# A depthwise 3x3 convolution in 64x64 tiles, its sums emptied by two engines, its order in a table of slots

## The chip, the cores and the metric

The kernel runs on one core of a Trainium2 chip. A core has five engines with a program of their own each, which meet at semaphores: TensorE (PE, matrix products into the accumulator memory PSUM), VectorE (DVE), ScalarE (ACT), GpSimd (POOL) and SyncE (SP), which starts transfers (DMA). Tensors that are worked on lie in SBUF, the on-chip memory with 128 partitions. The metric is the device time of one launch in microseconds (us), the median of several runs. Beside these runs one execution was taken by the hardware profiler; views and line numbers (L1471 is line 1471 of the kernel before) come from it.

## The reference

The input x has 4 samples of 256 channels and 48x48 points, in fp32. Four layers follow, each of the form x = x + layer(group norm of x): attention with 8 heads, a gate from large depthwise convolutions, single-head attention with a batch norm over all samples, and layer 3, which the change is in:

```python
def _L3_conv_ref(x, attn_w1, attn_w2, refine_w, refine_b):
    p = jnp.mean(x, axis=(2, 3))
    h = jax.nn.leaky_relu(p @ attn_w1.T, SLOPE)
    a = jax.nn.sigmoid(h @ attn_w2.T)
    y = x * a[:, :, None, None]
    y = conv(y, refine_w, padding='SAME', groups=C)      # 3x3, each channel by itself
    y = y + refine_b[None, :, None, None]
    mu = jnp.mean(y, axis=(2, 3), keepdims=True)
    var = jnp.mean(jnp.square(y - mu), axis=(2, 3), keepdims=True)
    y = (y - mu) * rsqrt(var + EPS)
    return jax.nn.leaky_relu(y, SLOPE)
...
x = x + _L2_conv_ref(_gn(x), ...)      # ends in W_w @ y, then the batch norm
x = x + _L3_conv_ref(_gn(x), ...)
```

## The kernel before

A sample has 256 channels, two channel halves (NK = 2) of 128 partitions each, and N = 2304 points. A *slice* is SL = 384 points (8 rows), six to a half (NSL), and a *third* is two slices, GW = 768 points (NG3 = 3). A *tile* of layer 3 is one half of one sample; there are eight, sample after sample in the order SEQ = 1, 2, 3, 0. Samples 1 to 3 lie in SBUF; sample 0 is loaded again into `x_back` (L1290).

Layer 2's last product needs statistics over all four samples, which `w_stats` (L1015) gathers while the attention still runs. So layer 3 begins by computing that product again and adding it to x. This is class `Pre`, in six *steps* per sample: four 64x64 products on TensorE (`product`, L1334), batch norm while ScalarE empties PSUM (`normed`, L1341), the addition to x (`gain`, L1365, mostly on GpSimd), statistics of the sum on VectorE (`stats`, L1370). Then `chain`: small operations on VectorE with four small products on TensorE between them and a reciprocal root on GpSimd (the helper `rsqrt`, L165), which give the group norm's mean and scale and the channel gate. They end in two ScalarE operations that write normed and gated x into a *pad*, a 50x50 image with a zero border (L1433). Four pads rotate.

Class `Conv` is one tile. `products` (L1458) does the first four taps of each slice on TensorE: the weight matrix is a 128x128 diagonal of one tap's weights (`diagonals`, L1045, made by GpSimd during layer 2), the other side a shifted window of the pad, and PSUM adds up. Two slices share a tile of two PSUM banks; three such tiles rotate (`two_banks`). `taps` (L1471) adds the other five taps, each a VectorE scalar_tensor_tensor (window times weight plus what PSUM holds) over a third, in place in PSUM. `evict` (L1477) adds the bias on ScalarE, writes the third `z` to SBUF and sums it. `centre` takes the first third's mean as a shift of origin, `square` (L1490) sums squares on ScalarE; `scales` (L1497 to L1505) are small VectorE operations and a `rsqrt` on GpSimd, `shift` (L1510) a 128x1 operation behind it; `scale` (L1516) norms z on ScalarE, `leak` (L1520) is the leaky relu on VectorE (z times slope, maximum with z: both inputs are z), `gain` (L1524) adds z to x on GpSimd in thirds, `store` (L1527) sends it out. In the last tile these four go third by third, gain on VectorE.

The order is written by hand: in this part of the program every engine executes its instructions as they stand in the code (`manual_schedule`), each behind the semaphore waits that the framework puts in for shared tiles. A loop over tiles and slices (from L1564) interleaves the work of three tiles: products of the present one, taps and norm of the one before, gain and store of the one before that, and one step or chain piece of a later sample. A judge of layer 0's sums (six small operations, value `sound`, read at the very end) stands ahead of it.

Of the kernel before, what the change touches and what calls it, by code (L numbers as in the profile page):

```python
# [9 lines left out]
F32 = mybir.dt.float32  # L10
# [4 lines left out]
P = 128  # L15
HW = 48
# [58 lines left out]
def usual_path(  # L75
# [958 lines left out]
    PE_TAPS = (0, 1, 2, 3)  # L1034
    DVE_TAPS = (4, 5, 6, 7, 8)
    diag = {}

    def diagonals():

        for k in range(NK):  # L1040
            xs = xsp.tile([P, NK, SL + 1], F32, tag="xs", name="diag")
            xs = xs.rearrange("p k s -> p (k s)")[:, : len(PE_TAPS) * P]
            diag[k] = xs.rearrange("p (t j) -> p t j", j=P)
            for n, t in enumerate(PE_TAPS):
                nc.gpsimd.tensor_scalar(  # L1045
                    diag[k][:, n, :], ident, rfw[:, k, t : t + 1], None, ALU.mult
                )
                yield 1
# [258 lines left out]

    W2 = HW + 2
# [5 lines left out]
    GW = 2 * SL  # L1314

# [5 lines left out]
    class Pre:  # L1321


        def __init__(self, n):
            self.n, self.b = n, SEQ[n]
            self.st = small.tile([P, NK, NSL, 6], F32, tag="gn_st", name="gn_st")
            self.steps = [(k, c) for k in range(NK) for c in range(L2C)]
# [25 lines left out]
        def add(self, i):  # L1353
            halves = [pj_tile()[:, :SL] for _ in range(2)]
            self.product(i, halves)
            tmp = wk.tile([P, 2, SL], F32, tag="tmp", name="tmp")
            for h in range(2):
                self.normed(i, tmp[:, h, :], halves[h])
            self.gain(i, tmp, nc.gpsimd)
# [7 lines left out]
        def stats(self, i):  # L1367
            k, c = self.steps[i]
            for s in (c, c + L2C):
                nc.vector.bn_stats(  # L1370
                    self.st[:, k, s, :], X[self.b][:, k, s * SL : (s + 1) * SL]
                )

        def chain(self):

            mv = small.tile([P, NK, 2], F32, tag="gn_mv", name="gn_mv")
            for k in range(NK):
                nc.vector.bn_aggr(mv[:, k, :], self.st[:, k].rearrange("p s f -> p (s f)"))
            yield
            ps = pj_tile()  # L1380
            nc.tensor.matmul(ps[:, 0:NK], lhsT=gmat, rhs=mv[:, :, 0], start=True, stop=True)
            yield
            gm = small.tile([P, NK], F32, tag="gn_gm", name="gn_gm")
            nc.vector.tensor_copy(gm, ps[:, 0:NK])
            dev = small.tile([P, NK], F32, tag="gn_dev", name="gn_dev")
            nc.vector.tensor_sub(dev, mv[:, :, 0], gm)
            sq = small.tile([P, NK], F32, tag="gn_sq", name="gn_sq")
            nc.vector.tensor_mul(sq, dev, dev)
            nc.vector.tensor_add(sq, sq, mv[:, :, 1])
            yield  # L1390
            ps = pj_tile()
            nc.tensor.matmul(ps[:, 0:NK], lhsT=gmat, rhs=sq, start=True, stop=True)
            yield
            gv = small.tile([P, NK], F32, tag="gn_gv", name="gn_gv")
            nc.vector.tensor_scalar(gv, ps[:, 0:NK], GN_EPS, None, ALU.add)
            rs = small.tile([P, NK], F32, tag="gn_rs", name="gn_rs", bufs=6)
            rsqrt(rs, gv)
            yield
            yield

            pm = small.tile([P, NK], F32, tag="pm", name="pm")
            nc.vector.tensor_mul(pm, dev, rs)
            nb = small.tile([P, NK], F32, tag="gn_nb", name="gn_nb", bufs=6)
            nc.vector.scalar_tensor_tensor(nb, gm, -1.0, rs, ALU.mult, ALU.mult)
            yield
            ps = pj_tile()
            for k in range(NK):
                nc.tensor.matmul(
                    ps[0:D, 0:1], lhsT=w1[:, k, :], rhs=pm[:, k : k + 1],
                    start=k == 0, stop=k == NK - 1,  # L1410
                )
            raw = small.tile([D, 1], F32, tag="hraw", name="hraw")
            nc.vector.tensor_copy(raw, ps[0:D, 0:1])
            hl = small.tile([D, 1], F32, tag="hl", name="hl")
            nc.vector.scalar_tensor_tensor(hl, raw, SLOPE, raw, ALU.mult, ALU.max)
            yield
            ps = pj_tile()
            for k in range(NK):
                nc.tensor.matmul(
                    ps[:, k : k + 1], lhsT=w2[:, k * P : (k + 1) * P], rhs=hl,  # L1420
                    start=True, stop=True,
                )

            ga = small.tile([P, NK], F32, tag="ga", name="ga")
            nc.scalar.activation(ga, ps[:, 0:NK], AF.Exp, scale=-1.0)
            nc.vector.tensor_scalar(ga, ga, 1.0, None, ALU.add)
            nc.vector.reciprocal(ga, ga)
            rsa = small.tile([P, NK], F32, tag="rsa", name="rsa")
            nc.vector.tensor_mul(rsa, rs, ga)
            nba = small.tile([P, NK], F32, tag="nba", name="nba")  # L1430
            nc.vector.tensor_mul(nba, nb, ga)
            for k in range(NK):
                nc.scalar.activation(  # L1433
                    pads[(self.n * NK + k) % NPAD][:, 1 : 1 + HW, 1 : 1 + HW],
                    X[self.b][:, k, :].rearrange("p (r c) -> p r c", c=HW), AF.Identity,
                    bias=nba[:, k : k + 1], scale=rsa[:, k : k + 1],
                )
                yield

    class Conv:  # L1440


        def __init__(self, i):
# [3 lines left out]
            self.z = big.tile([P, N], F32, tag="qk"[i // 2 % 2], name="z")  # L1447

            self.st = small.tile([P, 2, NG3], F32, tag="in_st", name="in_st", bufs=3)
            self.ps = {}  # L1450

        def products(self, s):
            g = s // 2
            if s % 2 == 0:
                self.ps[g] = two_banks(self.i * NG3 + g)
            for n, t in enumerate(PE_TAPS):
                dr, dc = divmod(t, 3)
                nc.tensor.matmul(  # L1458
                    self.ps[g][:, s % 2, :SL].rearrange("p (r c) -> p r c", c=HW),
                    lhsT=diag[self.k][:, n, :],  # L1460
                    rhs=self.pad[:, s * RS + dr : (s + 1) * RS + dr, dc : dc + HW],
                    start=n == 0, stop=n == len(PE_TAPS) - 1,
                )

        def taps(self, g):
            z = self.ps[g][:, :, :SL].rearrange("p h (r c) -> p h r c", c=HW)
            for t in DVE_TAPS:
                dr, dc = divmod(t, 3)
                r0 = 2 * g * RS + dr
                src = self.pad[:, r0 : r0 + 2 * RS, dc : dc + HW]  # L1470
                nc.vector.scalar_tensor_tensor(  # L1471
                    z, src.rearrange("p (h r) c -> p h r c", h=2),
                    rfw[:, self.k, t : t + 1], z, ALU.mult, ALU.add,
                )

        def evict(self, g):
            nc.scalar.activation(  # L1477
                self.z[:, g * GW : (g + 1) * GW].rearrange("p (h s) -> p h s", h=2),
                self.ps[g][:, :, :SL], AF.Identity, bias=vec[:, V_RB, self.k : self.k + 1],
                accum_out=self.st[:, 0, g : g + 1],  # L1480
            )
# [53 lines left out]


    ok = lp.tile([P, 2, LW], F32, name="ok")
    nc.vector.tensor_scalar(ok[:, 0, :], lsum, SUM_HI, None, ALU.is_le)
    nc.vector.tensor_scalar(ok[:, 1, :], lmin, SUM_LO, None, ALU.is_ge)
    okm = lp.tile([P, 1], F32, name="okm")  # L1540
    nc.vector.tensor_reduce(okm, ok, AX.XY, ALU.min)
    ps = pj_tile()
    nc.tensor.matmul(ps[0:1, 0:1], lhsT=okm, rhs=ones[:, 0:1], start=True, stop=True)
    sound = lp.tile([1, 1], mybir.dt.int32, name="sound")
    nc.vector.tensor_scalar(sound, ps[0:1, 0:1], P - 0.5, None, ALU.is_ge)

    pres = {0: Pre(0), 1: Pre(1)}
    for i in range(NK * L2C):
# [3 lines left out]
    pres[0].stats(NK * L2C - 1)  # L1552
    _drain(pres[0].chain())


    steps = {}
    for s in range(NSL):
        steps[0, s] = (1, s)
    for b in range(2, B):
        for c in range(L2C):  # L1560
            steps[NK * (b - 2) + 1, 2 * c] = (b, c)
            steps[NK * (b - 1), 2 * c] = (b, L2C + c)

    convs, pending = [], None  # L1564
    for i, (b, k) in enumerate(TILES):
        cv = Conv(i)
        convs.append(cv)
        prev = convs[i - 1] if i else None
# [912 lines left out]
```

## Time and profile before

| what | value |
|---|---|
| median of 3 runs | 3684.39 us (3683.62 to 3686.41) |
| the profiled execution | 3686.69 us |
| its span | 3685.0 us |
| granted TensorE clock, mean | 0.982 |
| first product of layer 3's convolution (L1458) | at 3454.75 us |
| last eviction (L1477) ends | at 3669.92 us |
| last gain (L1524) ends | at 3679.67 us |
| mean of one tap on VectorE (L1471, 128x768) | 1.02 us |

The span is the time from the first to the last record of the profiled execution. A row of the table of groups gives line, engine, operation, output<-inputs with shapes, count, then total busy time in us and mean in ns, and after the second bar the idle time before such operations with what ended it. "The chain" is the work that ended last, followed back from the end. "The waits" add up how long an engine stood for another.

### The profile page before, as it was taken

To read this page: it belongs to the slowest core of one execution; us is meant where nothing else is said; L and a number is where in the kernel's file an instruction comes from. 1 tells how busy PE (TensorE), PEld (TensorE's weight loads), DVE (VectorE), ACT (ScalarE), POOL (GpSimd) and SP (SyncE) were. 2 spreads that over 40 slices of the span, in tenths; PEclk is the share of its full clock that TensorE was granted. 3 is DMA by queue.
4 is the path that set the end of the run, shared out by engine and by line. 5 is a ranking of instruction groups with operands and counts; after the bars stand their busy time and mean duration, and the time that the engine had idled before them with its cause. 6 is when DMAs were issued, how large, how long until landed. Compare 5 with 4: busy or idle time off the path is not lost.

```text
span 3685.0 us, 86525 instructions
## 1 busy us (share of the span) xinstructions
PE 3516.1 (95%) x36338; PEld 1766.9 (48%) x36338; DVE 2520.1 (68%) x3209; ACT 2343.6 (64%) x3814; POOL 1423.6 (39%) x899
## 2 busy tenths in 40 slices
PE   8999999999999999999999999999999999999685
PEld 4554545554444444544444445444444445654343
DVE  3455555476778676767786667667967787576687
ACT  4565666566875885568758856687587555555353
POOL 2333333333343334333433343334333456664232
PEclk9999999999999999999999999999999999999797
DMA  2111111111111111311111111111111100000001
GB/s 90 47 26 22 26 21 25 21 29 18 26 21 25 21 25 21 76 21 25 21 25 21 25 21 25 21 25 21 25 17 25 17 6 6 6 8 4 26 34 70
DMA packets 112959, 95.53 MB, mean 26 GB/s; under 512 B 56128, under 2 KB 110000, under 8 KB 110768
## 3 DMA queue, kind: packets, MB, share of 16 engines
q1 hardware_dynamic: 109952, 87.73, 13.0%
q8 instruction: 286, 4.69, 0.5%
q10 hardware_dynamic: 2608, 2.18, 0.2%
q14 instruction: 113, 0.93, 0.1%
HBM read 56.97 MB, written 11.80 MB: 19 GB/s over the span
## 4 chain that ended last, share of the span: by engine, by line
PE 71%; DVE 14%; issue 6%; ACT 5%; POOL 4%; DMA 1%; SPq 0%; DVEq 0%; ACTq 0%; POOLq 0%
PE sc L246 27%; PE av L266 27%; PE pj L528 6%; DVE acc L292 5%; PE pj L610 3%; PE pj L559 3%; POOL half L277 2%; DVE sc L1471 2%; ACT pt L252 2%; PE pj L299 1%; ACT prod L789 1%; DVE av L1471 1%; PE pj L851 1%; DVE acc L286 1%; PE pj L967 1%
## 5 line engine op out<-in xcount | busy, mean ns | idle before, releaser
L252 ACT ACTIVATE pt<-sc 128x768 f32<-128x768 f32 x1944 | 1476.4, 812 | 790.0 <-PE sc L246 787.5
L277 POOL TENSOR_TENSOR half<-pt 128x768 f32<-128x768 f32 x477 | 939.9, 1972 | 1729.0 <-ACT pt L252 1650.1
L246 PE MATMUL sc<-q,k 64*64 64x384 f32 x13824 | 1280.1, 485 | 9.8 <-ACT pt L252 9.4
L266 PE MATMUL av<-pt,v 64*64 64x384 f32 x13824 | 1280.4, 485 | 0.0
L292 DVE TENSOR_TENSOR acc<-acc,pt 128x768 f32<-128x768 f32 x792 | 885.2, 1118 | 84.4 <-DVE acc L292 2.3
L246 PEld LDWEIGHTS sc<-q,k 64*64 64x64 f32 x13824 | 510.1, 133 | 636.2 <-issue 498.7
L266 PEld LDWEIGHTS av<-pt,v 64*64 64x64 f32 x13824 | 514.7, 133 | 590.7 <-issue 554.8
L292 DVE TENSOR_TENSOR acc<-acc,half 128x768 f32<-128x768 f32 x459 | 473.6, 1032 | 349.2 <-POOL half L277 348.3
L615 DVE SCALAR_TENSOR_TENSOR x<-pj,bo,x 128x384 f32<-128x384 f32 x192 | 118.2, 616 | 512.3 <-PE pj L610 512.0
L789 ACT ACTIVATE prod<-pd,wt 128x256 f32<-128x256 f32 x486 | 280.9, 745 | 0.2
L528 PE MATMUL pj<-xs,w 128*128 128x384 f32 (+1 forms) x720 | 275.4, 505 | 0.0
L347 POOL TENSOR_TENSOR o<-o,rinv 128x384 f32<-128x384 f32 x95 | 125.9, 1326 | 238.7 <-DMA rinv<-rinv 224.5
L528 PEld LDWEIGHTS pj<-xs,w 128*128 128x128 f32 x720 | 124.1, 189 | 127.9 <-issue 38.3
L610 PE MATMUL pj<-o,wo 128*128 128x384 f32 x384 | 160.7, 503 | 22.1 <-DVE x L615 17.9
L266 PE MATMUL av<-pt,qv 64*64 64x384 f32 x1728 | 174.6, 497 | 0.0
L246 PE MATMUL sc<-qv,kd 64*64 64x384 f32 x1728 | 169.7, 486 | 2.4 <-ACT pt L252 2.4
L807 DVE TENSOR_REDUCE prod<-prod 128x256 f32<-128x1280 f32 x114 | 168.6, 1479 | 0.0
L559 PEld LDWEIGHTS pj<-w,xs 128*128 128x128 f32 x1080 | 134.5, 191 | 24.1
L286 DVE TENSOR_TENSOR acc<-pt 128x768 f32<-128x768 f32 x99 | 131.7, 1331 | 12.5 <-ACT pt L252 12.5
L559 PE MATMUL pj<-w,xs 128*128 128x128 f32 x1080 | 134.9, 275 | 0.0
L544 ACT ACTIVATE k<-pj,bias 128x384 f32<-128x384 f32 x90 | 52.2, 580 | 106.6 <-PE pj L528 106.2
L343 POOL TENSOR_TENSOR o<-raw 128x384 f32<-128x384 f32 x95 | 112.2, 1182 | 0.0
(235 smaller groups left out, 2716.6 us busy)
## 6 DMA issues: line engine op xcount, KB each, us to landing
xs<-in_x_dram SPq DMA_DIRECT2D x90, 384.0 KB
rinv<-rinv SPq DMA_DIRECT2D x208, 94.5 KB
out_dram<-x SPq DMA_DIRECT2D x6, 1152.0 KB
l<-row SPq DMA_DIRECT2D x416, 1.5 KB
w<-in_wqkv_dram SPq DMA_DIRECT2D x32, 192.0 KB
x<-in_x_dram SPq DMA_DIRECT2D x5, 1152.0 KB
rinv<-ls SPq DMA_DIRECT2D x208, 1.5 KB
x_out<-x SPq DMA_DIRECT2D x6, 384.0 KB
```

Source lines behind the costliest of these rows:

```text
L246: nc.tensor.matmul(ps[c * D : (c + 1) * D, h, :SL], lhsT=u["of"]["k"][r, j0 : j0 + D], rhs=u["of"]["q"][r, u["qc"]], start=True, stop=True,)
L252: nc.scalar.activation(pt, ps[:, :, :SL], AF.Exp, scale=u["scale"])
L266: nc.tensor.matmul(u["av"][h * D : (h + 1) * D, half, :SL], lhsT=value(u, j, h)[r], rhs=pt[r, h, :], start=j == 0, stop=j == JB - 1,)
L277: nc.gpsimd.tensor_add(half, pts[0], pts[1])
L286: nc.vector.tensor_add(u["acc"], ready[0], ready[1])
L292: nc.vector.tensor_add(u["acc"], u["acc"], term)
L347: eng.tensor_mul(o, o, u["rinv"])
L528: nc.tensor.matmul(ps[:, :n], lhsT=at["w"][:, k, t, :], rhs=xs[s][:, k, :n], start=k == 0, stop=k == NK - 1,)
L559: nc.tensor.matmul(ps[:, i * P : (i + 1) * P], lhsT=xs[s][:, k, i * P : (i + 1) * P], rhs=at["w"][:, k, 2, :], start=k == 0, stop=k == NK - 1,
L610: nc.tensor.matmul(ps[:, :SL], lhsT=wo[:, p, k * P : (k + 1) * P], rhs=o["o"], start=True, stop=True,)
L789: nc.scalar.activation(bufs[n % 3][:, :, min(n, 1) + i].rearrange("p (r c) -> p r c", c=AS), pd[:, PAD + dr : PAD + dr + AS, PAD + dc : PA ...
L807: nc.vector.tensor_reduce(to, bufs[n % 3][:, :, : min(n, 1) + len(taps)], AX.X, ALU.add)
```

## The change

Eight taps (all but the middle one, tap 4) go to TensorE, as 64x64 products: four per pair of taps, one from each half of the partitions to each half. A slice now fills a two-bank tile by itself: bank h holds what came from partition half h, even-numbered taps in the same half of the partitions, odd-numbered ones in the other half. So a channel's sum lies in two places, one of them in the other half of the partitions, and emptying brings them together.

`evict(s)` empties one slice with four operations on 64 partitions: twice VectorE (middle tap times window plus one bank, into z) and twice ScalarE (the other bank plus bias, into `part`, at the other half of the partitions). `join(g)` adds `part` to z over a third and sums it in one tensor_tensor_reduce on VectorE. For the crossed halves a second bias tile `rb_x` is loaded with its halves exchanged. Diagonals are 128x64 and sixteen, from `ident2` (two identities of 64 on top of each other).

The order of all work is a table: `at(t, rank, fn)` puts a function into slot t, one slot per slice, and each slot's functions are issued by rank: FRONT, PRODUCT, CONV, EVICT, SMALL, NEXT, THEN, LAST, OUT. With t the first slot of a tile, its products stand at t to t+5, evictions one slot later, joins at t+3, +5, +7, squares at t+4, +6, +8, scales at t+9, shift at t+10, then scale, leak, gain and store in thirds, two slots apart (the last tile: one). Pads are written in thirds of 17, 16 and 15 rows (`ROWS`). The chain's small products go to columns from SL on of the present slice's first bank (`columns`), in place of tiles of their own. Three steps of the second sample move into the first sample's chain (`FILLED`), and the judge moves to slots 6 and 7.

The chain's operations are the same as before, only split into functions, and `judge` likewise; both bodies are left out here.

```diff
-    PE_TAPS = (0, 1, 2, 3)
-    DVE_TAPS = (4, 5, 6, 7, 8)
+    PE_TAPS, DVE_TAP = (0, 1, 2, 3, 5, 6, 7, 8), 4
     diag = {}
 
     def diagonals():
 
         for k in range(NK):
             xs = xsp.tile([P, NK, SL + 1], F32, tag="xs", name="diag")
-            xs = xs.rearrange("p k s -> p (k s)")[:, : len(PE_TAPS) * P]
-            diag[k] = xs.rearrange("p (t j) -> p t j", j=P)
+            xs = xs.rearrange("p k s -> p (k s)")[:, : len(PE_TAPS) * D]
+            diag[k] = xs.rearrange("p (t j) -> p t j", j=D)
             for n, t in enumerate(PE_TAPS):
                 nc.gpsimd.tensor_scalar(
-                    diag[k][:, n, :], ident, rfw[:, k, t : t + 1], None, ALU.mult
+                    diag[k][:, n, :], ident2, rfw[:, k, t : t + 1], None, ALU.mult
                 )
...
+    rb_x = lp.tile([P, NK], F32, name="rb_x")
+    for to, fr in zip(HALVES, HALVES[::-1]):
+        nc.sync.dma_start(rb_x[to, :], vecs[fr, V_RB, :])
...
+    ROWS = [0, 2 * RS + 1, 4 * RS + 1, HW]
...
-        def add(self, i):
-            halves = [pj_tile()[:, :SL] for _ in range(2)]
-            self.product(i, halves)
-            tmp = wk.tile([P, 2, SL], F32, tag="tmp", name="tmp")
+        def multiply(self, i):
+            self.halves = [pj_tile()[:, :SL] for _ in range(2)]
+            self.product(i, self.halves)
+
+        def evict(self, i):
+            self.tmp = wk.tile([P, 2, SL], F32, tag="tmp", name="tmp")
             for h in range(2):
-                self.normed(i, tmp[:, h, :], halves[h])
-            self.gain(i, tmp, nc.gpsimd)
+                self.normed(i, self.tmp[:, h, :], self.halves[h])
...
+            return [
+                (means, lambda ps: of_groups(ps, of["mv"][:, :, 0])),
+                (squares, lambda ps: of_groups(ps, of["sq"])),
+                (inverse, None), (pooled, first), (hidden, second), (gate, scaled),
+            ]
+        def pad(self, k, i):
+
+            r0, r1 = ROWS[i], ROWS[i + 1]
+            nc.scalar.activation(
+                pads[(self.n * NK + k) % NPAD][:, 1 + r0 : 1 + r1, 1 : 1 + HW],
+                X[self.b][:, k, :].rearrange("p (r c) -> p r c", c=HW)[:, r0:r1, :],
+                AF.Identity, bias=self.nba[:, k : k + 1], scale=self.rsa[:, k : k + 1],
+            )
...
-            self.ps = {}
+            self.ps, self.part = {}, {}
+
+        def window(self, r, s, t):
+            dr, dc = divmod(t, 3)
+            return self.pad[r, s * RS + dr : (s + 1) * RS + dr, dc : dc + HW]
 
         def products(self, s):
+            if s == 0:
+                self.z = big.tile([P, N], F32, tag="qk"[self.i // 2 % 2], name="z")
+
+                self.st = small.tile([P, 2, NG3], F32, tag="in_st", name="in_st", bufs=3)
+            now["ps"] = self.ps[s] = two_banks(self.i * NSL + s)
+            last = len(PE_TAPS) // 2 - 1
+            for n in range(last + 1):
+                for h, r in enumerate(HALVES):
+                    for e in range(2):
+                        nc.tensor.matmul(
+                            self.ps[s][HALVES[h ^ e], h, :SL].rearrange(
+                                "p (r c) -> p r c", c=HW
+                            ),
+                            lhsT=diag[self.k][r, 2 * n + e, :],
+                            rhs=self.window(r, s, PE_TAPS[2 * n + e]),
+                            start=n == 0, stop=n == last,
+                        )
+
+        def evict(self, s):
+
+
+
             g = s // 2
             if s % 2 == 0:
-                self.ps[g] = two_banks(self.i * NG3 + g)
-            for n, t in enumerate(PE_TAPS):
-                dr, dc = divmod(t, 3)
-                nc.tensor.matmul(
-                    self.ps[g][:, s % 2, :SL].rearrange("p (r c) -> p r c", c=HW),
-                    lhsT=diag[self.k][:, n, :],
-                    rhs=self.pad[:, s * RS + dr : (s + 1) * RS + dr, dc : dc + HW],
-                    start=n == 0, stop=n == len(PE_TAPS) - 1,
-                )
-
-        def taps(self, g):
-            z = self.ps[g][:, :, :SL].rearrange("p h (r c) -> p h r c", c=HW)
-            for t in DVE_TAPS:
-                dr, dc = divmod(t, 3)
-                r0 = 2 * g * RS + dr
-                src = self.pad[:, r0 : r0 + 2 * RS, dc : dc + HW]
+                self.part[g] = wk.tile([P, 2, SL], F32, tag="part", name="part")
+            z = self.z[:, s * SL : (s + 1) * SL].rearrange("p (r c) -> p r c", c=HW)
+            for h, r in enumerate(HALVES):
                 nc.vector.scalar_tensor_tensor(
-                    z, src.rearrange("p (h r) c -> p h r c", h=2),
-                    rfw[:, self.k, t : t + 1], z, ALU.mult, ALU.add,
-                )
-
-        def evict(self, g):
-            nc.scalar.activation(
-                self.z[:, g * GW : (g + 1) * GW].rearrange("p (h s) -> p h s", h=2),
-                self.ps[g][:, :, :SL], AF.Identity, bias=vec[:, V_RB, self.k : self.k + 1],
-                accum_out=self.st[:, 0, g : g + 1],
+                    z[r], self.window(r, s, DVE_TAP), rfw[r, self.k, DVE_TAP : DVE_TAP + 1],
+                    self.ps[s][r, h, :SL].rearrange("p (r c) -> p r c", c=HW),
+                    ALU.mult, ALU.add,
+                )
+                nc.scalar.activation(
+                    self.part[g][HALVES[1 - h], s % 2, :], self.ps[s][r, 1 - h, :SL],
+                    AF.Identity, bias=rb_x[r, self.k : self.k + 1],
+                )
+
+        def join(self, g):
+            z = self.z[:, g * GW : (g + 1) * GW]
+            nc.vector.tensor_tensor_reduce(
+                z, z, self.part[g].rearrange("p h s -> p (h s)"), 1.0, 0.0, ALU.add, ALU.add,
+                self.st[:, 0, g : g + 1],
             )
...
+    pres = [Pre(n) for n in range(B)]
+    STEPS = NK * L2C
+    for i in range(STEPS):
         pres[0].first(i, (nc.vector, nc.gpsimd)[i % 2])
         if i:
             pres[0].stats(i - 1)
-    pres[0].stats(NK * L2C - 1)
-    _drain(pres[0].chain())
-
-
-    steps = {}
-    for s in range(NSL):
-        steps[0, s] = (1, s)
-    for b in range(2, B):
-        for c in range(L2C):
-            steps[NK * (b - 2) + 1, 2 * c] = (b, c)
-            steps[NK * (b - 1), 2 * c] = (b, L2C + c)
-
-    convs, pending = [], None
-    for i, (b, k) in enumerate(TILES):
-        cv = Conv(i)
-        convs.append(cv)
-        prev = convs[i - 1] if i else None
-        older = convs[i - 2] if i > 1 else None
-        final = i == len(TILES) - 1
-        rest = iter(())
+    pres[0].stats(STEPS - 1)
+
+    FILLED = 3
+    filled = iter(range(FILLED))
+    for n, part in enumerate(pres[0].chain()):
+        part[0](None)
+        if part[1]:
+            part[1](pj_tile())
+        if n in (1, 2, 4):
+            pres[1].first(next(filled), nc.gpsimd)
+    for i in range(NG3):
+        pres[0].pad(0, i)
...
+    FRONT, PRODUCT, CONV, EVICT, SMALL, NEXT, THEN, LAST, OUT = range(9)
+    events = {}
+
+    def at(t, rank, fn):
+        events.setdefault(t, []).append((rank, fn))
...
+    def columns():
+
+        return now["ps"][:, 0, SL:]
+
+    def put_chain(t, parts):
+        for dt, (head, tail) in enumerate(parts):
+            at(t + dt, FRONT, lambda fn=head: fn(None))
+            if tail:
+                at(t + dt, SMALL, lambda fn=tail: fn(columns()))
+
+    def put_step(t, n, i, gap=1):
+        at(t, PRODUCT, lambda: pres[n].multiply(i))
+        at(t, NEXT, lambda: pres[n].evict(i))
+        at(t, OUT, lambda: pres[n].gain(i, pres[n].tmp, nc.gpsimd))
+        at(t + gap, LAST, lambda: pres[n].stats(i))
+
+    for i in range(NG3):
+        at(2 + i, LAST, lambda i=i: pres[0].pad(1, i))
+    for i in range(FILLED):
+        at(i // 2, LAST, lambda i=i: pres[1].stats(i))
+    for i in range(FILLED, STEPS):
+        put_step(i - FILLED, 1, i)
+    put_chain(6, judge())
+    SAMPLE = NK * NSL
+    for n in range(1, B):
+        t = (n - 1) * SAMPLE
+        if n > 1:
+            for i in range(STEPS):
+                put_step(t - 9 + 2 * i, n, i)
+        put_chain(t + 4, pres[n].chain())
+        for k in range(NK):
+            for i in range(NG3):
+                at(t + 10 + k * NSL + 2 * i, LAST, lambda n=n, k=k, i=i: pres[n].pad(k, i))
+
+    def put_tile(t, cv, final):
         for s in range(NSL):
+            at(t + s, CONV, lambda s=s: cv.products(s))
+            at(t + s + 1, EVICT, lambda s=s: cv.evict(s))
+        for g in range(NG3):
+            at(t + 2 * g + 3, NEXT, lambda g=g: cv.join(g))
+            at(t + 2 * g + 4, THEN, lambda g=g: cv.square(g))
+        at(t + 3, THEN, cv.centre)
+        at(t + 9, THEN, cv.scales)
+        at(t + 10, FRONT, cv.shift)
+        for g, cols in enumerate(THIRDS):
+            t0, dt = (t + 10 + g, 1) if final else (t + 11 + 2 * g, 2)
+            at(t0, THEN, lambda cols=cols: cv.scale(cols))
+            at(t0 + 1, NEXT, lambda cols=cols: cv.leak(cols))
+            eng = nc.vector if final else nc.gpsimd
+            at(t0 + 1 + dt, OUT, lambda cols=cols: cv.gain(cols, eng))
+            at(t0 + 1 + dt, OUT, lambda cols=cols: cv.store(cols))
+
+    for i in range(len(TILES)):
+        put_tile(i * NSL, Conv(i), i == len(TILES) - 1)
+    for t in range(max(events) + 1):
+        for _, fn in sorted(events.get(t, ()), key=lambda job: job[0]):
+            fn()
```

## The prediction

> **What bounds the kernel now.** I read the page first, for the whole program, and then only the stretch that the change touches.
>
> ```profile
> PE 3516.1 (95%) x36338; PEld 1766.9 (48%) x36338; DVE 2520.1 (68%) x3209; ACT 2343.6 (64%) x3814; POOL 1423.6 (39%) x899
> PE 71%; DVE 14%; issue 6%; ACT 5%; POOL 4%; DMA 1%; SPq 0%; DVEq 0%; ACTq 0%; POOLq 0%
> ```
>
> TensorE carries the program up to about 3417 us (attention). Layer 3's convolutions begin at 3454.75 (the first L1458 matmul) and the span ends at 3685.0. The change can move 231 us, and in those the limit is another one. The table of engine busy time by stretch, the longest chain and the groups, all from 3454 to 3685:
>
> ```profile
> 3540.00:3560.00 20.00, 15.31 (x54) 7.96 (x55) 16.91 (x37) 8.02 (x13) 8.36 (x6) 0.83 0.06 23
> sum 231.00, PE 168.42 PEld 87.30 DVE 181.34 ACT 103.29 POOL 76.12; mean PE 14.03 PEld 7.27 DVE 15.11 ACT 8.61 POOL 6.34
> ```
>
> ```profile
> by line: DVE sc L1471 26.3%; DVE av L1471 17.5%; DVE z L1520 9.0%; issue 7.0%; PE sc L1458 5.7%; ACT z L1477 4.5%; DVE gn_st L1370 3.6%; ACT junk L1490 3.3%; POOL x L1365 3.2%; ACT pad L1433 2.0%; ACT tmp L1341 2.0%; POOL x_back L1365 1.6%;
> ...
> 3454.75 5.46 PE sc L1458 x8
> ```
>
> ```profile
> L1471 DVE SCALAR_TENSOR_TENSOR sc<-pad,rfw,sc 128x768 f32<-128x768 f32 x80 | 81.6, 1020 | 2.3
> L1471 DVE SCALAR_TENSOR_TENSOR av<-pad,rfw,av 128x768 f32<-128x768 f32 x40 | 40.6, 1016 | 1.1
> L1524 POOL TENSOR_TENSOR x<-x,z 128x768 f32<-128x768 f32 x18 | 32.4, 1813 | 0.0
> L1341 ACT ACTIVATE tmp<-pj,bi,sc 128x384 f32<-128x384 f32 x36 | 21.9, 658 | 12.8 <-PE pj L1334 12.8
> L1520 DVE SCALAR_TENSOR_TENSOR z<-z 128x2304 f32<-128x2304 f32 x7 | 18.6, 2660 | 0.0
> L1477 ACT ACTIVATE z<-sc,vec 128x768 f32<-128x768 f32 x16 | 14.4, 898 | 56.5 <-DVE sc L1471 50.2 <-PEq L2407 6.3
> L1510 DVE SCALAR_TENSOR_TENSOR in_mr<-in_mv,in_ri 128x1 f32<-128x1 f32 x8 | 7.2, 899 | 0.7 <-POOL in_ri L165 0.7
> ```
>
> In the first, columns after the stretch are its length and the busy time of PE, weight loads, VectorE, ScalarE and GpSimd with counts, then the clock. VectorE is busy 181 of 231 us and taps are 44% of the chain, 122 of them in the five taps (120 x 1.02), and ScalarE idles 85 us waiting for taps. The last row is odd: a 128x1 operation at 0.9 us, which takes 0.16 in the tail. The timelines of GpSimd and VectorE at 3553 show why:
>
> ```profile
> 3553.49 1.81 POOL L1524 TENSOR_TENSOR x<-x,z 128x768 f32<-128x768 f32 x1
> ```
> ```profile
> 3553.75 1.57 DVE L1510 SCALAR_TENSOR_TENSOR in_mr<-in_mv,in_ri 128x1 f32<-128x1 f32 x1
> ```
>
> Both end together, at 3555.3.
>
> **What the Trainium skill says.** "SBUF — State Buffer", Who interferes with whom: a VectorE instruction with two SBUF inputs and a GpSimd instruction that reads SBUF exclude each other; the later one is blocked for the whole of the earlier. The trace agrees (above; the leak at 3565.66 takes 3.22 us and the leak at 3513.67, without a neighbour, 2.46). "PSUM — Partial Sum Buffer", PSUM bank collisions raise a hardware error: order is needed between two engines in one bank and quadrant, reads included. No trace here shows a collision; what matters is that such order becomes semaphore waits. "TensorEngine Tiling (Array Packing)", PSUM Bottleneck: tiling speeds the matmuls, not the emptying of PSUM. No run here shows it yet.
>
> **The change, part by part.** TensorE: 4 matmuls of 128x128 per slice (2.85 us) become 16 of 64x64, four at a time. The chain has eight records of L1334, 64x64 products too, in 1.24 us at full clock, 0.16 each: 2.5 a slice, and 0.9 more with a layer-2 step (four products): at most 3.5.
>
> The rows that price the emptying, from the page:
>
> ```profile
> L615 DVE SCALAR_TENSOR_TENSOR x<-pj,bo,x 128x384 f32<-128x384 f32 x192 | 118.2, 616 | 512.3 <-PE pj L610 512.0
> L544 ACT ACTIVATE k<-pj,bias 128x384 f32<-128x384 f32 x90 | 52.2, 580 | 106.6 <-PE pj L528 106.2
> ```
>
> VectorE: 120 taps go (120 x 1.056 with gaps = 127). It gets 96 operations 64x384 on PSUM and SBUF; the nearest row is L615's: 96 x 0.65 = 62. ScalarE loses 24 evictions (24 x 1.09 = 26) and gets 96 of 64x384 with one bias pointer, as L544: 96 x 0.62 = 60. VectorE also gets 24 joins, 128x768 with a sum, which no row shows. Below: the L1524 VectorE addition, 0.957, plus about 0.19 for reading the sum (L1477's accumulator read). Above: half rate, which "DVE Microarchitecture" gives for scalar_tensor_tensor with two SBUF sources not in bf16: 1.9. But the leak is such an operation and takes 0.955 for 768 elements, so I take 1.12. Totals: VectorE 181 - 127 + 62 + 27 = 143, ScalarE 103 - 26 + 60 = 137. If the engines ran side by side, 3.1 us a slice would do.
>
> They don't. The built program's waits for one slice read: VectorE's first half waits for TensorE; ScalarE's first half waits for VectorE's first; VectorE's second waits for ScalarE's first; ScalarE's second waits for VectorE's second. The order is by tile, though at one moment they would be in different banks. So a slice is a chain of four: 0.656 + 0.62 + 0.656 + 0.62 (each 0.04 for the hand-over, as 0.03 to 0.05 between engines in the trace). Only after its second half is VectorE free for other work, while ScalarE does its own second. The period of a slice is therefore 0.62 + 0.656 + the larger of (0.656 + VectorE's other work) and (0.58 + ScalarE's other work). Other work: step eviction 1.14 (L1341 pair less overlap), square 1.05, scale third 0.95, pad third 0.96; join 1.15, leak third 0.985, stats 1.03, scales 1.0 with rsqrt 0.55.
>
> Kinds of slices, from the table of slots:
> - after an even slot, ScalarE has square and pad: 1.28 + 0.58 + 2.01 = 3.87; with leak and stats on VectorE, 3.95.
> - after an odd slot with a step (eviction and scale third): 3.95; without a step join alone counts: 3.08.
> - seven slots after scales: 5.1 to 5.7, because join, scales, rsqrt, shift stand in line.
> - the first slices: 5.2 for the products at half clock (5.46 now) then 1.9, and 3.1 to 4.8 where chain and judge stand in front.
> Added over 48 slots: 197 us, from the first product to the last eviction. Before, this was 3669.92 - 3454.75 = 215.2. So without anything more the change gains 18 us here.
>
> Lock: shift is in front of a slice's eviction, and in POOL's order a gain comes right behind the rsqrt on which it waits. The gain starts first, and shift waits 1.76, seven times: 12.3. In slots 14 to 26, where both steps and thirds give POOL gains, five leaks meet one, up to 1.41 each: 0 to 7, I take 3.5. Now all of it is on the chain, since the chain has no slack. 197 + 15.8 = 212.8.
>
> Start: three steps of the next sample move into the first chain. GpSimd has a gain of 1.81 ahead of rsqrt's slot and the gate stands behind an eviction: +4.0 and +2.3, less 1.3 for the first pad in thirds: +5.1. The first three products move ahead of the last w_stats (L1015): about -3.0. First product at 3454.75 + 2.1 = 3456.85. Two tiny loads on SP for rb_x follow x_back and are long done; 8 more diagonals on POOL fall into waits of 2.3 to 4.3 us before its halves, free; without that cover they would cost about 0.6 to 1.4 each, 5 to 11 us. Stores go out in thirds, 24 for 12 in all, on SP, where nothing else waits behind them. The small products in a slice's bank wait for nothing new: their reader stands at the front of the next slot, and the bank comes round three slots later. The judge's 0.9 us move from the start to slots 6 and 7, where they are counted.
>
> Tail: now 9.75 from the last eviction to the last gain. It gains a join (1.12) and leaks of the tile before (0.985, partly in the wait) for 12; the blocked shift adds 1.8: 13.8. The last store takes 5.33 as now.
>
> Sum: 3456.85 + 212.8 + 13.8 + 5.3 = 3688.8, against this execution's span of 3685.0: +3.8, or +0.1%. The execution was 3686.69 in all; the median of the runs is 3684.39, so 3688.2; I round to 3689 because gaps in issue among some 450 operations are counted nowhere.
>
> **Rivals.**
> (a) *The lock is not felt.* VectorE's shift gets the port first because it waits on the same rsqrt, and leaks miss the gains. For: the hand-over (0.04) is no longer than GpSimd's own gap. Against: of eight shifts of before, seven average 1.0 us. Then 197 and 12: 3671 on the span, 3670 (-0.4%).
> (b) *Slower by the chain's links.* 192 links and 24 joins are now in a row. A hand-over with 0.1 in place of 0.04 costs, summed over the slots, 7 us; 0.15 costs 12.6; a join of 1.9 costs 14. A hand-over of about 0.07 is where "slower" decides. For: waits in a row leave no slack, and operations on half the partitions have no row. Against: hand-overs are measured. 3701 for the join or 0.15.
> (c) *The engines overlap after all*, another order of issue than I read: 35 us less, about 3650. Against: the waits are explicit.
> (d) *TensorE becomes the bound*: its gaps are 0.4 to 1.4 us a slot; if the clock fell to half (0.5 in the stretch 3454 to 3460), a slot would take 5.2 and the end come 60 later. It keeps 0.83 to 1.0 in later stretches with longer gaps. Hardly.
> That the change doesn't do what it says: the matmuls and table are there; the side by side emptying isn't, and that is my main case.
>
> **How the numbers follow.** Main case, 3689: 0.48, own range 3680 to 3700. (a) 0.17, (b) 0.27, (c) 0.05, (d) 0.03. A measurement tells about 0.2%, 7.4 us, from no change: 3677 to 3692. The main case falls by 0.02 below that, 0.29 within and 0.17 above. (a) and (c) are faster, (b) and (d) nearly all slower (0.02 of (b) within). Faster 0.24, same 0.31, slower 0.45. The range leaves out (c), (d), and the ends of (a) and (b): 3664 to 3709.
>
> **What would show it.** Right: in the timeline of a slice VectorE and ScalarE alternate and never overlap within it; waits of ScalarE for VectorE's z and of VectorE for ScalarE's part lead the table of waits; most slots 3.9 us; shift at 1.5 to 1.9 us beside a GpSimd gain; first product near 3457; last eviction near 3670. Wrong: overlapping halves; joins at 1.9; shifts of 0.16; TensorE below 0.6 clock in the loop.

## The result and the profile after

The changed kernel takes 3689.07 us (median of 4 runs, 3686.38 to 3691.23), the kernel before 3685.40 (4 runs). The ratio is 1.001 with a 95% interval of 0.9993 to 1.0027: no difference that can be measured, 0.1% slower at the most likely. The prediction was 3689.0.

The profiled execution of the changed kernel has a span of 3684.7 us, a little less than the 3685.0 of before. This doesn't contradict the medians: the unchanged part ended earlier in it. The last reciprocal of the attention (L357, the same line in both kernels) starts at 3414.67 us, and at 3418.65 in the execution of before. So I measure all traces from that point, in three stretches: to the first product of the convolution, from there to the end of the last eviction, and from there to the end of the span.

| kernel | L357 to first product | to last eviction | to the end | sum |
|---|---|---|---|---|
| before | 36.1 | 215.2 | 15.0 | 266.3 |
| changed | 41.2 | 208.6 | 20.2 | 270.0 |

The loop gained 6.6 us; start and end lost 5.1 each. The sum, +3.7, is what the medians show.

The page's busy times differ from those of before by less than 2%, and so say little:

```profile
PE 3513.0 (95%) x37490; PEld 1747.7 (47%) x37490; DVE 2503.4 (68%) x3247; ACT 2386.2 (65%) x3889; POOL 1424.6 (39%) x907
```

The table of busy time by stretch from 3454 to 3685 (columns as before: PE, weight loads, VectorE, ScalarE, GpSimd) says more. VectorE went from 181 to 161 us, ScalarE from 103 to 144, and no engine is full:

```profile
sum 231.00, PE 163.90 PEld 73.01 DVE 160.80 ACT 144.31 POOL 72.54; mean PE 13.66 PEld 6.08 DVE 13.40 ACT 12.03 POOL 6.04
```

The table of waits of the changed kernel in the same stretch tells where they stand (us, times, longest):

```profile
ACT part L1516 <- DVE z L1511: 69.9, 69, 4.0
...
DVE z L1511 <- ACT part L1516: 45.4, 48, 1.8
```

Each engine waits for the other, 115 us in all. The timelines of one slice (3597.26 to 3599.79) and what follows it show the pattern: VectorE, then ScalarE, then VectorE, then ScalarE, and no two of the four at once. In all 48 slices the third and the fourth start 0.03 to 0.04 us after the one before has ended. (A line gives start, duration, engine, line of the kernel, operation and count; in brackets stand the idle time before it and what ended it.)

```profile
3597.26 0.60 DVE L1511 SCALAR_TENSOR_TENSOR z<-pad,rfw,sc 64x384 f32<-64x384 f32 x1
3598.56 0.62 DVE L1511 SCALAR_TENSOR_TENSOR z<-pad,rfw,sc 64x384 f32<-64x384 f32 x1 [0.70 <-ACT part L1516]
3599.21 0.96 DVE L1565 SCALAR_TENSOR_TENSOR z<-z 128x768 f32<-128x768 f32 x1
3601.95 0.61 DVE L1511 SCALAR_TENSOR_TENSOR z<-pad,rfw,av 64x384 f32<-64x384 f32 x1 [1.79 <-ACT ga L1444]
```
```profile
3597.95 0.57 ACT L1516 ACTIVATE part<-sc,rb_x 64x384 f32<-64x384 f32 x1 [0.32 <-DVE z L1511]
3599.21 0.58 ACT L1516 ACTIVATE part<-sc,rb_x 64x384 f32<-64x384 f32 x1 [0.69 <-DVE z L1511]
3599.82 0.93 ACT L1535 ACTIVATE junk<-z,in_c 128x768 bf16<-128x768 f32 x1
```

The groups of the changed kernel from 3417 on give the prices:

```profile
L1511 DVE SCALAR_TENSOR_TENSOR z<-pad,rfw,sc 64x384 f32<-64x384 f32 x64 | 39.2, 612 | 35.4 <-ACT part L1516 29.1 <-PE sc L1493 5.6
L1516 ACT ACTIVATE part<-sc,rb_x 64x384 f32<-64x384 f32 x64 | 36.9, 576 | 53.9 <-DVE z L1511 53.4
L1565 DVE SCALAR_TENSOR_TENSOR z<-z 128x768 f32<-128x768 f32 x24 | 31.0, 1296 | 1.6 <-ACT z L1561 1.0
L1523 DVE CUSTOM_DVE_ANT_0 z<-z,part 128x768 f32<-128x768 f32 x24 | 23.0, 957 | 0.6
L1555 DVE SCALAR_TENSOR_TENSOR in_mr<-in_mv,in_ri 128x1 f32<-128x1 f32 x8 | 14.1, 1757 | 4.6 <-POOL in_ri L165 4.6
```

VectorE's halves take 0.612 us (0.616 was taken), ScalarE's 0.576 (0.58). So half the partitions cost as much as all: the rows priced before the change, with 128 partitions, were 0.616 and 0.580. The join is the custom operation L1523, 0.957, and its accumulator read adds 0.08: not the 1.9 of the upper bound. That bound came from the Trainium skill, "Vector Engine (DVE) Microarchitecture Reference", Points that are easy to get wrong, which halves the throughput of scalar_tensor_tensor with two such inputs; the leak is such an operation and takes 0.955 undisturbed, no longer than the join, so no run here shows the halving. The shift (L1555) takes 1.76 us in every one of its eight executions. Here is one, VectorE first and then GpSimd:

```profile
3607.03 1.75 DVE L1555 SCALAR_TENSOR_TENSOR in_mr<-in_mv,in_ri 128x1 f32<-128x1 f32 x1 [0.69 <-POOL in_ri L165]
```
```profile
3606.44 0.55 POOL L165 TENSOR_TENSOR in_ri<-in_ve,mhalf 128x1 f32<-128x1 f32 x1 [10.86 <-DVE in_c L1531]
3606.96 1.80 POOL L1569 TENSOR_TENSOR x<-x,z 128x768 f32<-128x768 f32 x1
```

The root ends at 3606.99. GpSimd's addition, next in its order, starts at 3606.96 and the shift at 3607.03; both end within 0.02 us of 3608.77. Both stood behind the same root, and in all eight places GpSimd's addition starts about 0.07 us ahead.

### The profile page after: what moved, and what is told of

Read it like the earlier page. It is cut to its first block, busy times and chain, and to the rows that moved or that the text cites. A ratio compares the mean times of both kernels' runs of the same rounds, so it can differ in the third digit from the quotient of the medians.

```text
span 3684.7 us, 88999 instructions
## 1 busy us (share of the span) xinstructions
PE 3513.0 (95%) x37490; PEld 1747.7 (47%) x37490; DVE 2503.4 (68%) x3247; ACT 2386.2 (65%) x3889; POOL 1424.6 (39%) x907
## 4 chain that ended last, share of the span: by engine, by line
PE 71%; DVE 13%; ACT 6%; issue 6%; POOL 3%; DMA 1%; DVEq 0%; SPq 0%; POOLq 0%; ACTq 0%
PE sc L246 27%; PE av L266 27%; PE pj L528 6%; DVE acc L292 5%; PE pj L610 3%; PE pj L559 3%; POOL half L277 2%; ACT pt L252 2%; PE pj L299 1%; ACT prod L789 1%; DVE z L1511 1%; ACT part L1516 1%; PE pj L851 1%; DVE acc L286 1%; PE pj L967 1%
## 5 line engine op out<-in xcount | busy, mean ns | idle before, releaser
L1493 PE MATMUL sc<-pad,diag 64*64 64x384 f32 x1024 | 105.7, 557 | 28.2 <-ACT pad L1464 25.9
```

## Experiments

Two theories carry the prediction. *The chain of four*: a slice is emptied by two engines in turn. *The port lock*: VectorE operations with two SBUF inputs are shut out by GpSimd additions. A third, smaller one is about the start. Each gets an edit of its own, then all go together, and three more runs ask what is left.

**The shift behind the eviction.**

```diff
-        at(t + 10, FRONT, cv.shift)
+        at(t + 10, THEN, cv.shift)
```

> The changed kernel with one word changed: the 128x1 shift of slot t+10 stands behind the slice's eviction on VectorE (rank THEN) and no longer in front of it. Theory of the port lock: shift waits 1.76 us for a GpSimd gain and about 0.6 for rsqrt, seven times on the chain of evictions; behind the eviction both are over by then. So 14 to 17 us less than the changed kernel, about 3673, and shift takes 0.16 us in the loop. Rival (VectorE's wait there is hidden, since ScalarE or TensorE is late anyway): within 3 us of the changed kernel. Rival (only the wait for rsqrt counts): 4 to 5 us less, and shift still at 1.76.

Measured: 3676.54 us (12 runs), ratio to before 0.9979 (0.9971 to 0.9988), against 1.001 for the changed kernel: 12 us less. The loop is 196.6 us, 12.0 less. The record of the line in this kernel gives the least, middle and longest duration:

```profile
L1555 DVE SCALAR_TENSOR_TENSOR in_mr<-in_mv,in_ri x8: 146/150/1762, 3500.1 to 3660.6; 128x1 f32<-128x1 f32 x8
```

The wait is on the path, and it is more than the wait for the root alone (4 to 5 us): both rivals fall. It is a little less than expected. The middle shift is down to 0.15 us, but two of the eight still take 1.76 (one of them behind the loop), and leaks rose from 31.0 to 33.1 us: where shift no longer waits, the next operation with two inputs meets an addition.

**The two engines one slot apart.** `evict` is split; the VectorE half keeps its name, the ScalarE half is `cross`. Number, size and content of the operations stay.

```diff
-            at(t + s + 1, EVICT, lambda s=s: cv.evict(s))
+            at(t + s + 1, EVICT, lambda s=s: cv.cross(s))
+            at(t + s + 2, EVICT, lambda s=s: cv.evict(s))
```

> The changed kernel, with ScalarE emptying a slice one slot after its products and VectorE two slots after, so that the two engines are in different PSUM tiles in the same slot and no wait stands between them; the number and size of operations stay. Theory of the chain of four: most slots fall from 3.9 us to the larger of VectorE's and ScalarE's own sums, about 3.3, so 22 to 28 us less than the changed kernel, about 3664; waits of ScalarE for VectorE's z (70 us) and of VectorE for ScalarE's part (45 us) fall below a quarter. Rival (TensorE and the pads set the pace): no more than 5 us less, about 3685, and the idle time moves to waits for TensorE.

Measured: 3648.67 us (4 runs), ratio 0.9902 (0.9887 to 0.9918). That is 40 us less than the changed kernel, and the loop is 169.2, 39.4 less. The mutual waits are gone: of VectorE's for `part` 0.6 us is left, of ScalarE's for the same slice's z nothing. These rows of the groups stand against those of the changed kernel with 35.4 and 53.9 us of idle time before; what ScalarE still waits for are products and small operations of the chains:

```profile
L1508 DVE SCALAR_TENSOR_TENSOR z<-pad,rfw,sc 64x384 f32<-64x384 f32 x64 | 39.2, 612 | 1.5 <-ACT part L1519 0.6
L1519 ACT ACTIVATE part<-sc,rb_x 64x384 f32<-64x384 f32 x64 | 36.9, 576 | 13.4 <-DVE gn_gm L1399 5.9 <-PE sc L1493 3.5 <-DVE hraw L1429 2.5
```

In the timelines (VectorE, then ScalarE) an engine's two halves now stand back to back, as one pair of 1.24 or 1.17 us, and the two engines are busy at the same time, in different slices:

```profile
3601.27 1.24 DVE L1508 SCALAR_TENSOR_TENSOR z<-pad,rfw,av 64x384 f32<-64x384 f32 x2
3602.54 0.96 DVE L1568 SCALAR_TENSOR_TENSOR z<-z 128x768 f32<-128x768 f32 x1
3603.53 1.24 DVE L1508 SCALAR_TENSOR_TENSOR z<-pad,rfw,sc 64x384 f32<-64x384 f32 x2
3604.81 1.41 DVE L1526 CUSTOM_DVE_ANT_0 z<-z,part 128x768 f32<-128x768 f32 x1
3606.15 0.08 DVE L1526 DVE_READ_ACCUMULATOR2_ANT in_st<- 128x1 f32 x1
3606.26 1.24 DVE L1508 SCALAR_TENSOR_TENSOR z<-pad,rfw,sc 64x384 f32<-64x384 f32 x2
```
```profile
3602.92 1.17 ACT L1519 ACTIVATE part<-sc,rb_x 64x384 f32<-64x384 f32 x2
3604.11 1.03 ACT L1564 ACTIVATE z<-z,in_mr,in_ri 128x768 f32<-128x768 f32 x1
3605.53 1.17 ACT L1519 ACTIVATE part<-av,rb_x 64x384 f32<-64x384 f32 x2 [0.38 <-PE av L1493]
```

The chain of four is shown; its price was larger than I expected (22 to 28). A rival that wasn't run by itself is that the extra slot only gives TensorE more time: but VectorE's evictions of the changed kernel waited 6 us in all for products, 4.9 of them at one place, so this can't be where 39 us come from. By the starts of VectorE's evictions, the first 26 slices take 97.5 us and not 115.6, 0.7 less a slice, near the 0.6 expected (3.9 to 3.3); the last 21 take 64.5 and not 84.9, 1.0 less. I had taken the larger of the two engines' sums slot by slot. Without mutual waits that is wrong: a full slot of one engine is made up in its next, emptier one, so the average counts. The slots above last 2.26 and 2.73 in turn, 2.5 on average, though ScalarE's work in every other one (pair, square, pad) is 3.2 where pads are still written.

**The first chain cleared.** Two steps in it in place of three, and their additions behind it, on VectorE:

```diff
-    FILLED = 3
+    FILLED = 2
...
-        if n in (1, 2, 4):
-            pres[1].first(next(filled), nc.gpsimd)
+        if n in (1, 3):
+            i = next(filled)
+            ps = two_banks(i)
+            pres[1].product(i, [ps[:, 0, :SL], ps[:, 1, :SL]])
+            early.append(wk.tile([P, 2, SL], F32, tag="tmp", name="tmp"))
+            pres[1].normed(i, early[i], ps[:, :, :SL])
+    for i in range(FILLED):
+        pres[1].gain(i, early[i], nc.vector)
...
-    put_chain(6, judge())
+    put_chain(7, judge())
...
-        put_chain(t + 4, pres[n].chain())
+        put_chain(t + (5 if n == 1 else 4), pres[n].chain())
```

> The changed kernel with the first sample's chain cleared: two steps of the second sample in it in place of three, their products behind the chain's small products, their additions on VectorE after the chain's last operation and not on GpSimd in it; the second sample's chain and the judge one slot later. Theory: rsqrt, pm, the gate and ga lose 4.2 + 1.6 + 1.8 + 1.65 us of waits for GpSimd's additions and for one eviction, and one product of 1.4 us stays in the way: the first product of the convolution 7 to 8 us earlier after the last attention product, and the end 6 to 8 us earlier, about 3682. Rival (the start is given back, because the evictions of the first slots get the work that was moved): less than 2 us.

Measured: 3682.91 us (13 runs), ratio 0.9995 (0.9987 to 1.0003), 5 to 6 us less than the changed kernel. The first product comes 33.3 us after L357 and not 41.2, 7.9 earlier as expected; the loop takes 211.5, 2.9 more, since one more step is now in its slots. So part is given back, but more than half stays. What stood in the chain of the changed kernel, VectorE's timeline first, then GpSimd's:

```profile
3440.79 0.16 DVE L1408 TENSOR_SCALAR gn_gv<-pj 128x2 f32<-128x2 f32 x1 [0.74 <-PE pj L1394]
3445.88 1.75 DVE L1415 TENSOR_TENSOR pm<-gn_dev,gn_rs 128x2 f32<-128x2 f32 x1 [4.93 <-POOL gn_rs L165]
...
3452.41 1.81 DVE L1448 TENSOR_SCALAR ga<-ga 128x2 f32<-128x2 f32 x1 [3.77 <-ACT ga L1444]
```
```profile
3443.38 1.81 POOL L1370 TENSOR_TENSOR x<-x,tmp 128x768 f32<-128x768 f32 x1 [6.26 <-ACT tmp L1345]
3445.14 0.71 POOL L165 TENSOR_TENSOR gn_rs<-gn_gv,mhalf 128x2 f32<-128x2 f32 x1
3445.81 1.81 POOL L1370 TENSOR_TENSOR x<-x,tmp 128x768 f32<-128x768 f32 x1
...
3452.40 1.81 POOL L1370 TENSOR_TENSOR x<-x,tmp 128x768 f32<-128x768 f32 x1 [4.79 <-ACT ga L1444]
```

The root waits for the first addition (input at 3440.95, start 3445.14), `pm` is shut out by the second (1.75 for 0.16), `ga` by the third (1.81 for 0.17).

**All three.** The three diffs together.

> The three edits together. Theory: the chain of evictions, the shift in front of it and the late start add up, since each stands on the path that sets the end: 14 to 17, 22 to 28 and 6 to 8 us, in all 42 to 53 less than the changed kernel, about 3641, a ratio to the kernel before of about 0.988. Rival (once the engines run side by side VectorE has slack, and shift and start are hidden): no better than the stagger alone by more than 8 us.

Measured: 3633.57 us (4 runs), ratio 0.9859 (0.9844 to 0.9874): 56 us less than the changed kernel, 50 less than before, or 1.4%. The parts add up (12 + 40 + 6 = 58). The rival, that shift and start would hide, falls: beyond the stagger alone there are 15 us. This is the version that beats both kernels.

| kernel | L357 to first product | to last eviction | to the end | sum |
|---|---|---|---|---|
| shift behind | 41.2 | 196.6 | 19.7 | 257.5 |
| one slot apart | 41.9 | 169.2 | 19.0 | 230.2 |
| chain cleared | 33.3 | 211.5 | 20.1 | 264.9 |
| all three | 33.3 | 163.3 | 18.6 | 215.3 |

**The shift on ScalarE**, on top of all three:

```diff
+            self.nm = small.tile([P, 1], F32, tag="in_nm", name="in_nm")
+            nc.vector.tensor_scalar(self.nm, mv[:, 0:1], -1.0, None, ALU.mult)
...
-            nc.vector.scalar_tensor_tensor(
-                self.mr, self.mv[:, 0:1], -1.0, self.ri, ALU.mult, ALU.mult
-            )
+            nc.scalar.activation(self.mr, self.nm, AF.Identity, scale=self.ri)
```

> The three edits together, and the shift no longer on VectorE: the negative mean is a 128x1 VectorE operation in scales, ahead of rsqrt, and ScalarE multiplies it by the root in slot t+10. In the three edits together shift still took 0.75 us on average (6.0 in all), twice at 1.75 because a GpSimd addition had begun. Theory of the port lock: ScalarE is not shut out, so 4 to 6 us go (4 in the loop, where VectorE is the fullest engine, 1.6 in the tail), to a ratio of about 0.9845 to before, and the ScalarE operation takes about 0.2 us each time also beside a GpSimd addition. Rival: GpSimd's addition slows any small operation of that moment, so that the ScalarE operation takes over 1 us and nothing is gained.

Measured: 3634.97 us (4 runs), ratio 0.9871 (0.9854 to 0.9887), the same as all three within their intervals; the sum from L357 is 215.4. ScalarE's operation takes 0.294 to 0.296 us all eight times, each time in the midst of a GpSimd addition, so it isn't shut out; there the theory holds and the rival falls. But the 4 to 6 us were not gained. (Of the shifts with all three edits not two but three had taken 1.75 to 1.78, two in the loop and one behind it.) The groups of this kernel show where the lock went:

```profile
L1568 DVE SCALAR_TENSOR_TENSOR z<-z 128x768 f32<-128x768 f32 x24 | 32.8, 1370 | 2.7 <-ACT z L1564 2.1
L1526 DVE CUSTOM_DVE_ANT_0 z<-z,part 128x768 f32<-128x768 f32 x24 | 31.2, 1299 | 0.8
```

A leak or join that meets nothing takes 0.955 and 0.957, 22.9 and 23.0 for 24. With all three edits joins were 27.6, leaks 32.1 and shifts 6.0 (1.3 undisturbed): 4.6 + 9.2 + 4.7 = 18.5 us above it. Now joins and leaks are 8.2 + 9.9 = 18.1 above. The 37 additions of GpSimd take 72.6 us in all, with all three edits 71.4, and another operation with two inputs waits for them. So here, where VectorE is nearly always busy, taking one victim away made others. This is read from one pair of traces; the sum is no constant (20.9 us in the changed kernel by the same count, 13.6 with the shift behind the eviction).

**Superfluous work**, on top of all three: 48 ScalarE operations in one kernel, 48 VectorE operations in another, both on a constant tile and without effect on the output.

```diff
+            at(t + s + 1, LAST, cv.idle)
...
+        def idle(self):
+            junk = lp.tile([P, GW], mybir.dt.bfloat16, tag="junk", name="junk4")
+            nc.scalar.activation(
+                junk[:, :SL], diag[0].rearrange("p t j -> p (t j)")[:, :SL], AF.Identity,
+                bias=vec[:, V_RB, 0:1],
+            )
```

In the other kernel `idle` is:

```diff
+            more = small.tile([P, 6], F32, tag="more", name="more")
+            nc.vector.bn_stats(more, diag[0].rearrange("p t j -> p (t j)")[:, :SL])
```

> The three edits together with 48 superfluous ScalarE operations, one a slot, 128x384 at about 0.55 us: 26 us of work. Theory (VectorE bounds the loop now, 18 to 19.5 of 20 us busy, ScalarE has 16 to 17): about a third to a half shows, 6 to 14 us more than the three edits. Rival (the two engines still take turns, so that every operation on either is on the path): 22 to 26 us more.

> The three edits together with 48 superfluous VectorE operations, one a slot, statistics of a constant 128x384 tile at about 0.55 us: 26 us of work. Theory (VectorE bounds the loop now): nearly all of it shows, 21 to 26 us more than the three edits. Rival (ScalarE or TensorE bounds it): less than 12.

Measured: 28.9 us of ScalarE work cost 11 us (3644.44, ratio 0.9895, 0.9875 to 0.9915); 26.4 us of VectorE work cost 17 (3650.36, ratio 0.9911, 0.9892 to 0.9931), each in two runs. The traces give less: from L357 to the end 9.8 and 13.6 us, the loops 10.8 and 13.6; the other 1.4 and 3.6 lie ahead of L357, where nothing was changed, and why is open. Either way the engines no longer take turns, or ScalarE's work would have cost 22 to 26 us. VectorE is the nearer bound but not the only one: its result lies between theory (21 to 26) and rival (below 12), by the trace nearer to the rival. About 7 us of the missing were taken from the lock: joins and leaks fell from 27.6 and 32.1 to 25.4 and 27.3 (while `pm` in the chains rose by 1.7), presumably because additions now fell beside the superfluous statistics, which have one input. In the stretch 3460 to 3600 of the kernel with all three edits, VectorE is busy 131 of 140 us, TensorE 130 and ScalarE 122: three limits close together. What each of the three is worth by itself was not settled.

## Why the prediction was right

Its steps against the trace of the changed kernel:

- *The slice as a chain of four*: right in kind and size. Measured between VectorE's second halves, an odd slot after square and pad lasts 3.80 to 3.88 us (3.87 predicted), slots with a step 4.03 to 4.05 (3.95), a slot behind a join alone 2.92 (3.08). Only 21 of the 47 lie between 3.7 and 4.1, though, not most.
- *The seven slots after scales*, lock included: 6.24 to 6.86, predicted 6.84 to 7.44. The shift's 1.76 was exact. The rest, 5.1 to 5.7 predicted, measured 4.5 to 5.1: the parts that the prediction gives for such a slot (0.62 + 0.66 + 0.66, join 1.15, scales 1.0, root 0.55) add up to 4.6 and were about right, but the slot was put about half a us higher than they make; over the seven about 4 us. This is nearly the whole difference of the loop, 208.6 against 212.8.
- *Leaks behind additions*: four leaks of the loop took 2.27 to 2.29 us and their slots 5.13 to 5.16 in place of 3.84 to 3.88, 5 us in all; a fifth, 1.53, cost its slot nothing. 3.5 was taken of 0 to 7. The undisturbed leak before the change lasts 2.54 us, not 2.46, which is what the chain counts of it.
- *The start*: predicted +2.1, measured +5.1. The products ahead of the last w_stats, with the judge out of their way, gave 3.2 (3.0 predicted), the pad in thirds 1.25 (1.3). The waits of the root and the gate came out as taken, 4.1 and 2.5 ("+4.0 and +2.3"). What failed is a term put at nothing: I had applied the port lock to the loop but not to the first chain, where `pm` and `ga` lost 1.6 each to the moved additions.
- *The tail*: 15.05 to the last addition, predicted 13.8. The shift was shut out as predicted; a leak was too, which wasn't counted:

```profile
3669.88 1.75 DVE L1555 SCALAR_TENSOR_TENSOR in_mr<-in_mv,in_ri 128x1 f32<-128x1 f32 x1 [0.75 <-POOL in_ri L165]
3671.55 0.95 DVE L1565 SCALAR_TENSOR_TENSOR z<-z 128x768 f32<-128x768 f32 x1
3672.72 3.35 DVE L1565 SCALAR_TENSOR_TENSOR z<-z 128x768 f32<-128x768 f32 x2 [0.23 <-ACT z L1561]
```

Two leaks in 3.35 us, 1.4 more than twice the undisturbed one, beside a GpSimd addition from 3672.58 to 3674.39.

- *TensorE off the path*: right, but its 2.5 us a slice (2.81 measured) came from a misreading. The eight records of L1334 are four products with two records each, and the clock was at half until 3460.90. "3.1 us a slice" for engines side by side is 143/48 = 3.0.

So the sum, 3689, owes its closeness to three misses that cancel: loop -4.2, start +3.0, tail +1.3. The mechanisms are shown, the match to the microsecond is luck. Nor was the outcome the likeliest by the prediction: no measurable change had 0.31, slower 0.45.

Of the rivals, (a) falls with shift at 1.76 in all eight places; (b) with the join at 0.957 and hand-overs of 0.03 to 0.05; (c) with the alternating timelines; (d) with a clock of 0.78 to 1.0 in the stretches from 3460 to 3670.

That the change brought nothing has one main cause: of its idea, two engines emptying a slice side by side, only the division was carried out. The semaphores that go with a shared PSUM tile made the halves wait for each other, and this cost 39 us of the loop; the version with the same operations one slot apart shows it.

## What to carry to other kernels

Two engines that read one PSUM tile may be made to take turns, whatever banks they read; look at the built waits, and if they alternate, let the engines be in different tiles at the same moment, one slot apart. When a chain of waits has no slack, a 0.15 us operation put in front of it can cost 1.8, so a small VectorE operation with two SBUF inputs doesn't belong right behind an event that also releases a GpSimd addition. Removing such a meeting paid where the operation stood on the path and VectorE had room (12 us); on the nearly full VectorE other operations took over the wait, and nothing was gained.

## What the hardware showed beside

A small `tensor_scalar` with one SBUF input and one constant was shut out as well: `ga` took 1.81 us for 0.17, from 3452.41 to 3454.22, while a GpSimd addition ran from 3452.40 to 3454.21. "SBUF — State Buffer", Who interferes with whom, of the Trainium skill counts tensor_scalar among operations that can take the shared ports in a two-port mode; the trace agrees. Operations of the same kind and size whose input lies in PSUM were not: `gn_gv` took 0.16 us in the midst of an addition three times (at 3514.42 with all three edits, at 3479.42 and 3521.96 one slot apart). The ScalarE operation beside an addition took 0.295 us throughout, as the page says of ScalarE. That the blocked time stayed at 18 us when the shift left VectorE, I had not expected.
